# Silu's products of two strips on 64x32 tiles, results out of PSUM by ScalarE and the residual by GpSimd, in the spline layer of a four-layer network

## The chip, the cores and the metric

One core of one Trainium2 chip runs the whole program. The metric is the device time of one execution in microseconds (us); lower is better. The kernel before was timed three times, and one execution was profiled.

## What is computed

The input x is 8 images of 16 channels, 256 x 256 pixels, float32. Four layers follow each other, each of the form x = x + layer(groupnorm(x)): a capsule convolution with three rounds of routing (layer 0), a spline convolution (layer 1), attention inside 16 x 16 patches (layer 2), and a circular 3 x 3 convolution (layer 3). The change lies in layer 1, whose core is this:

```python
patches = _extract_patches(x, 3, 1, 1)          # 3x3, zero padding, x normalised
bspl = _b_splines(patches, grid)                # 8 cubic basis functions of every value
base_w = base_weight.sum(axis=2)
spl_w = (spline_weight * spline_scaler[..., None]).sum(axis=2)
out = einsum('bjhwn,ijn->bihw', silu(patches), base_w)
out = out + einsum('bjhwns,ijns->bihw', bspl, spl_w)
out = out + bias_weight[None, :, None, None]
```

So every output row needs two kinds of products with 3 x 3 weights: those of silu(x), with 16 channels, and those of the eight basis functions of x. Then a bias and the residual x are added, and the sums for the next layer's normalisation are taken.

## The kernel before, in words

**Staging.** The layers run one after another; the images between them lie in DRAM. Layer 1 (`layer1`, L851) goes over 8 images with 16 strips each; a strip is 16 rows, 128 strips in all, numbered i = 16 b + j. The result of a strip lies in one PSUM bank: four groups (n) of 32 partitions, each with 2 rows x 16 output channels, by two halves (k) of 256 pixels, so 4 x 2 x 2 = 16 rows.

**Features** (`features`, L986). A DMA fetches the rows of a strip, eight pairs of rows, into `xr`, each value four times, so that 128 partitions hold 2 rows x 16 channels x 4 shifts (L994, 1 MB). For four pairs at a time: ScalarE takes a distance to the middle of a spline and folds it (`d`, L1012, L1015); VectorE clips it twice (`a` and `e`, L1023); ScalarE squares both into PSUM (`sq`, L1029); VectorE multiplies to cubes (L1032); GpSimd subtracts the two cubes into the ring `bases` (L1041); and VectorE makes the second half, the same values kept only right of the middle (L1044). Rows outside the image are set by L1049. The ring has three places; a strip's products need its own place and the first pair of the next one. The last strip of an image has a ninth pair.

**Silu** (`silus`, L1063). Three DMAs fetch eight rows each with the 16 channels, 256 KB: `rs` twice, for the rows above and below (r = 0 and 2), and `res`, the residual (r = 1). ScalarE makes silu of both `rs` (L1082) into two of four tiles `silu`. Each holds 8 rows x 16 channels on its 128 partitions; the two together cover the rows that the strip's outputs need.

**Products** (`conv_strip`, L1098). Everything goes through the one matmul at L1106, with 32 output columns, so that four products (n = 0 to 3) go to four groups of 32 PSUM partitions. For each of two q, two kinds and three dx there are four spline products of K = 128; then three dx with four silu products (L1136), whose weights `wm` have 128 rows with zeros where a row doesn't matter for the output pair n. A float32 product is two records in the trace, so a strip has 108 spline records (some cover only half of the pixels) and 24 silu records.

**Results.** VectorE adds PSUM, bias and residual into `y`, in two halves of 256 columns (L1143), turned to the order in which layer 2 reads patches (runs of 16 pixels). It then takes the sums for the normalisation (L1155), and a DMA stores `y` (L1158).

**Order of the work.** The engines' queues are filled in program order, and that order comes from a planner written out in the kernel (`_Order`, L188). Each step is given to it with an engine, an estimated time, what it reads and writes, and a `lag` until its result is there (for DMAs); `mode="shared"` marks steps of VectorE and GpSimd that it never lets overlap; on TensorE it adds 0.25 for a change of mode. It has the number of buffers of each kind, looks at four sets of steps ahead (a set is the features of strip n, the products of strip n - 1, the silus of strip n, and what `ahead` adds), and takes the step that can start first, by rank: the set's number times the period (13.3 here) less the time to the end of its chain. Nothing of this is decided on the chip. In particular a step that waits holds back everything behind it in its engine's queue.

**The start** (`prepare`, L924). Spline weights `sw`, their scales `sc`, silu's weights `main` (nine copies to be summed) and the bias `b1` are fetched at L933 into ring places that are not used yet; VectorE scales (L937), TensorE sums over nine taps (L945 for splines, L970 for silu), VectorE finishes `tw` (L954 to L966), ScalarE copies `wm` (L982). The lags given are 10 and 16 us for these loads, 13 for the first `xr` and 6 for the others, 16 for the residual and silu rows of strip 0 and 4 for all others. In set 2 the weights of layer 2 are fetched (L1171, L1172).

**The end.** Layer 2 begins with `attend` (L1453): VectorE makes `t` (L1456) out of a patch that was loaded ahead, GpSimd adds the embedding (L1460). `t` comes from the pool `mid`, which takes over memory of layer 1's pools.

## Time and profile before

| what | value |
|---|---|
| three runs | 7644.09, 7646.63, 7649.12 us; median 7646.63 us |
| profiled execution, own time | 7643.24 us |
| its span | 7641.5 us |
| busy in the span | PE 6889.0, DVE 5415.1, ACT 2691.9, POOL 3248.8 us |
| in 5000 to 5700 us (layer 1) | PE 655.5, DVE 594.5, ACT 504.1, POOL 291.2 us, DMA 0.48 |
| layer 1's matmuls (L1106) | 4368.8 to 6132.2 us |
| one silu group of a strip | 24 records, 2.8 us |
| L1143, 128x256 | 477 ns each, two per strip |
| L1041, 128x1024 on GpSimd | 2888 ns mean |
| VectorE waiting for L1041, 4400 to 6130 us | 29.9 us |

PE is TensorE (PEld its weight loads), DVE VectorE, ACT ScalarE, POOL GpSimd and SP the engine whose queue issues most DMAs. Busy is the sum of the durations of an engine's instructions. A wait "A <- B" is time that the engine of A stood idle, ended by B. TensorE's records are pipelined, so what a group costs is read from start to start, not from durations. A duration on VectorE or GpSimd contains the time in which the instruction stood still for the other engine.

### The profile page before, as it was taken

The page shows a single profiled execution, that of the slowest core. Times are in us where ns is not written, and L with a number is a line of the kernel's source. Part 1 is how long each engine was busy: PE and PEld are TensorE (multiplying, and loading weights), DVE is VectorE, ACT ScalarE, POOL GpSimd, SP SyncE. Part 2 cuts the span into 40 slices and gives each one's busy share as a digit, 9 for nine tenths or more (in the row PEclk, how much of TensorE's full clock was granted, in tenths as well). Part 3 has the DMA queues.
Part 4 walks back from the last instruction along what each step waited for, and adds up shares of the span by engine and source line. Part 5 has one row for each costly group of instructions (what it writes and reads, how often), then busy time and mean ns, then how long its engine had stood idle before and what let it go on. Part 6 is the DMA issues. An engine that isn't in the chain of part 4 may idle for free.

```text
span 7641.5 us, 105946 instructions
## 1 busy us (share of the span) xinstructions
PE 6889.0 (90%) x43144; PEld 3276.6 (43%) x43144; DVE 5415.1 (71%) x6462; ACT 2691.9 (35%) x3835; POOL 3248.8 (43%) x1884
## 2 busy tenths in 40 slices
PE   4888888999898999998998499999999999999999
PEld 1333333333333333333333254554545566666634
DVE  5768888887888888888888688888888833333322
ACT  1222222222222222222222277777777712111200
POOL 0545555555555555555555444444444411111100
PEclk9999999999999999999999699999999999999999
DMA  6222222222222222222221344444445533333276
GB/s 243 67 65 76 77 77 77 77 77 77 77 77 77 77 77 77 77 77 76 77 76 50 105 153 156 153 152 152 154 151 161 159 114 97 86 85 97 68 214 189
DMA packets 451065, 813.01 MB, mean 106 GB/s; under 512 B 57490, under 2 KB 299282, under 8 KB 415250
## 3 DMA queue, kind: packets, MB, share of 16 engines
q1 hardware_dynamic: 380946, 738.85, 33.6%
q10 hardware_dynamic: 69632, 67.39, 3.0%
q8 instruction: 340, 5.57, 0.3%
q14 instruction: 147, 1.20, 0.1%
HBM read 595.63 MB, written 211.03 MB: 106 GB/s over the span
## 4 chain that ended last, share of the span: by engine, by line
PE 51%; POOL 21%; DVE 16%; issue 4%; ACT 3%; DMA 3%; SPq 0%; POOLq 0%; DVEq 0%; ACTq 0%
PE ps L1106 13%; POOL dd L765 11%; POOL s L765 8%; PE cv L545 8%; PE pqk L1466 6%; DVE dd L756 4%; PE p3s L1577 4%; PE cv L549 4%; PE pl L654 3%; PE po L1493 3%; PE pv L1473 3%; PE psc L1481 3%; PE fb L622 3%; DMA xr<-x1p 2%; POOL s L810 2%
## 5 line engine op out<-in xcount | busy, mean ns | idle before, releaser
L765 POOL TENSOR_TENSOR dd<-dd 128x1024 f32<-128x1024 f32 x512 | 1206.2, 2356 | 1594.9 <-DVE dd L756 1575.0
L1106 PE MATMUL ps<-bases,tw 128*32 128x512 f32 (+1 forms) x13824 | 1377.8, 550 | 109.6 <-DVE bases L1049 92.0
L756 DVE SCALAR_TENSOR_TENSOR dd<-rb,v 128x1024 f32<-128x1024 f32 (+1 forms) x1024 | 1075.2, 1082 | 206.7 <-PE rb L745 196.8
L554 ACT COPY v<-cv 128x1024 f32<-128x1024 f32 x512 | 518.2, 1012 | 1909.2 <-PE cv L549 1909.2
L1041 POOL TENSOR_TENSOR bases<-e,a 128x1024 f32<-128x1024 f32 (+1 forms) x264 | 744.9, 2823 | 1044.5 <-DVE e L1032 922.0
L545 PE MATMUL cv<-kt,w 128*128 128x512 f32 x2048 | 1090.9, 658 | 38.0 <-DVE dd L756 26.5
L1106 PEld LDWEIGHTS ps<-bases,tw 128*32 128x32 f32 x13824 | 732.4, 109 | 764.9 <-issue 458.3
L644 DVE TENSOR_TENSOR pr<-v,fb 128x2048 f32<-128x2048 f32 (+1 forms) x512 | 1019.5, 2014 | 24.9 <-PE pl L654 20.0
L745 PE MATMUL rb<-rs,ct_fold 32*128 32x512 f32 x3584 | 796.5, 658 | 8.3 <-ACT rs L727 2.7
L765 POOL TENSOR_TENSOR s<-s,dd 128x512 f32<-128x512 f32 x512 | 652.2, 1274 | 29.9
L545 PEld LDWEIGHTS cv<-kt,w 128*128 128x128 f32 x2048 | 366.1, 199 | 598.4 <-issue 389.7
L549 PE MATMUL cv<-kt,w 64*128 64x512 f32 x2048 | 590.9, 654 | 0.0
L654 PE MATMUL pl<-pr,ct_fold 128*32 128x512 f32 x3584 | 525.9, 610 | 61.0 <-DVE pr L644 60.3
L1460 POOL TENSOR_TENSOR t<-t,emb 128x512 f32<-128x512 f32 x128 | 162.1, 1266 | 961.9 <-DVE t L1456 950.8
L622 PEld LDWEIGHTS fb<-f,ct_fold 128*128 128x128 f32 x3072 | 376.7, 195 | 340.7 <-issue 296.7
L622 PE MATMUL fb<-f,ct_fold 128*128 128x128 f32 x3072 | 436.3, 290 | 90.7 <-DVE f L608 88.4
L1466 PE MATMUL pqk<-w_qk,t 128*128 128x512 f32 x1024 | 484.4, 596 | 7.6 <-POOL t L1460 7.6
L765 POOL TENSOR_TENSOR s<-v,dd 128x512 f32<-128x512 f32 x256 | 328.9, 1285 | 319.4 <-DVE dd L756 319.2
L1477 ACT ACTIVATE vt<-pv,w_b2v 128x128 f32<-128x128 f32 x512 | 146.0, 367 | 841.2 <-PE pv L1473 810.8
L1497 DVE TENSOR_TENSOR y<-po,res 128x512 f32<-128x512 f32 x128 | 88.5, 691 | 487.6 <-PE po L1493 487.6
L745 PEld LDWEIGHTS rb<-rs,ct_fold 32*128 32x128 f32 x3584 | 241.2, 188 | 380.7 <-DVE dd L756 211.7
L1032 DVE TENSOR_TENSOR e<-e,sq 128x1024 f32<-128x1024 f32 (+1 forms) x264 | 314.5, 1191 | 95.4 <-ACT sq L1029 95.4
(254 smaller groups left out, 8995.6 us busy)
## 6 DMA issues: line engine op xcount, KB each, us to landing
kt<-d SPq DMA_DIRECT2D x256, 516.0 KB
xr<-x1p SPq DMA_DIRECT2D x120, 1024.0 KB
rs<-x SPq DMA_DIRECT2D x256, 256.0 KB
d<-dn ACTq DMA_DIRECT2D x64, 516.0 KB
xs<-in_x_dram SPq DMA_DIRECT2D x16, 2048.0 KB
xs<-in_x_dram SPq DMA_DIRECT2D x64, 512.0 KB
res<-in_x_dram SPq DMA_DIRECT2D x64, 512.0 KB
x<-s SPq DMA_DIRECT2D x128, 256.0 KB
```

The lines of the kernel that those rows point to most:

```text
L545: nc.tensor.matmul(ps()[:, n], w[:, 0, j, :], t[:, a : a + 2, 0:W], start=True, stop=False)
L549: nc.tensor.matmul(ps()[:, n], w[at, 1, j, :], t[at, a : a + 2, 2 - n : 2 - n + W], start=False, stop=True)
L554: nc.scalar.copy(v[h]()[:, 4 * g : 4 * g + 4, j * W : j * W + W], ps().rearrange("p n (a w) -> p (n a) w", w=W),)
L622: nc.tensor.matmul(fb()[:, k * P : k * P + P], unfold[:, h, k, :], f()[:, 3], start=True, stop=True)
L644: nc.vector.tensor_tensor(pr()[:, :n], v[h]()[:, 4 * g : 4 * g + n], p().unsqueeze(1).to_broadcast([P, n, 512]), ALU.mult,)
L654: nc.tensor.matmul(pl()[at : at + 32], sel[:, g, h, :], pr()[:, t, :], start=h == 0 and g == 0, stop=h == 1 and (g == 1 or t == 3),)
L745: nc.tensor.matmul(r()[:, n], spread[at, g, h, :], rs()[at], start=True, stop=True)
L756: nc.vector.scalar_tensor_tensor(dd()[:, :n], r()[:, :n], 1.0 / B, v[h]()[:, a : a + n], ALU.subtract, ALU.mult)
L765: op("POOL", us, lambda: nc.gpsimd.tensor_tensor(out[0](), a[0](), b[0](), ALU.add), a[1] + b[1], out[1])
L1041: nc.gpsimd.tensor_tensor(v, rows(part(e)), rows(part(a)), ALU.subtract)
L1106: nc.tensor.matmul(out if k is None else out[:, k], lhs, rhs, start=start, stop=stop, skip_group_check=True)
L1466: nc.tensor.matmul(ps, t[:, n, k * P : (k + 1) * P], wqk[:, n, :], start=n == 0, stop=n == 1)
```

## The change

Six things, all in one edit:

1. *Silu's products in pairs of strips.* Weights `wm` are 64 rows, stored twice (partitions 0 to 63 and 64 to 127), without n: four rows of image x 16 channels are enough for a pair of output rows. At every odd strip the silu products of it and of the even strip before it are issued together: three dx with eight matmuls each, K = 64 rows by 32 columns, which alternate between the even strip's PSUM bank and the odd strip's, and between the two halves of the partitions. For the odd strip the `rs` rows are fetched with halves swapped, by two DMAs of 128 KB each, so that the two strips use opposite halves. The even strip's spline products stand before this group and the odd strip's behind it.
2. *Results.* Instead of L1143, ScalarE moves PSUM with the bias to `y` in one activation of 128 x 512, and GpSimd adds the residual in one addition of 128 x 512. The even strip's result leaves PSUM after the silu group, the odd strip's after its spline products.
3. *First loads.* The first `xr` is put ahead of the weights; the planner's costs of first loads on SP are 2.8, 3.5, 1.8 and 1.2 with lag 3 or 8 instead of 0.5 with lags of 10 to 16, and strip 0's rows have the lag of all others. `main` is a quarter as large.
4. *wm* is copied out by VectorE instead of ScalarE.
5. *Layer 2's weights* are fetched in set 6 instead of set 2.
6. *`t` of layer 2* comes from a pool of its own, opened first in layer 2.

The planner's period is 12.4 instead of 13.3. The mask `keep` for the silu rows outside the image follows the swapped halves. The core of the diff:

```diff
-            wm = one.tile([P, 3, 4, 2 * C], F32, name="wm")
+            wm = one.tile([P, 3, 2 * C], F32, name="wm")
...
-            order = _Order({**places, **banks}, 13.3)
+            order = _Order({**places, **banks}, 12.4)
...
-                sw, sc, main = at2[:, :2592], at2[:, 2592:3888], at1[:, :3456]
+                sw, sc, main = at2[:, :2592], at2[:, 2592:3888], at1[:, :864]
...
+                first = dict(sw=3.5, sc=1.8, main=1.2, b1=0.5)
                 for name, t in (("sw", sw), ("sc", sc), ("main", main), ("b1", b1)):
-                    op("SP", 0.5, lambda name=name, t=t: nc.sync.dma_start(out=t, in_=self.d[name]), [], [(name,)], lag=16.0 if name == "main" else 10.0)
+                    op("SP", first[name], lambda name=name, t=t: nc.sync.dma_start(out=t, in_=self.d[name]), [], [(name,)], lag=3.0)
...
-                op("ACT", 0.5, lambda: nc.scalar.copy(wm.rearrange("p d n m -> p (d n m)"), ps()[:, 512:896]), [(ps, 1)], [("wm",)])
+                def finish_main():
+                    nc.vector.tensor_copy(wm.rearrange("p d m -> p (d m)"), ps()[:, 512:608])
+
+                op("DVE", 0.2, finish_main, [(ps, 1)], [("wm",)], mode="shared")
...
-                op("SP", 0.5, fetch, [], [(xr, 0)], lag=6.0 if i else 13.0)
+                op("SP", 0.5 if i > 2 else 2.8, fetch, [], [(xr, 0)], lag=6.0 if i else 8.0)
+                if not i:
+                    prepare(op)
...
+                        swap = i % 2 and r != 1
+                        for at, row, n in ((0, r + 4, 4), (64, r, 4)) if swap else ((0, r, 8),):
+                            nc.sync.dma_start(
+                                out=to()[at : at + 16 * n].rearrange("p k w -> p (k w)"),
+                                in_=self.x1[j, b, :, row : row + n].rearrange("c r k w -> r c (k w)"),
+                            )
+
+                    op("SP", 0.5 if i else 0.7, fetch, [], [(to, 0)], lag=4.0)
...
+                if i % 2:
+                    both = [(open_ps.pop(k), k) for k in (i - 1, i)]
+                    keys = [("s", k, n) for k in range(2) for n in range(2)]
+                    for dx in range(3):
+
+                        def silus(dx=dx):
+                            for n in range(4):
+                                for p, k in both:
+                                    half = n // 2 ^ k % 2
+                                    at = slice(64 * half, 64 * half + 64)
+                                    src = sring[k % 2 * 2 + n % 2]
+                                    mm(n, None, wm[at, dx], src[at, :, dx : dx + W], bool(k % 2 and not dx), dx == 2 and not k % 2, p)
+
+                        op("PE", 0.9, silus, [("wm",), *keys], [(p, 0) for p, _ in both], mode="r64")
+                    evict(b, j - 1, both[0][0], op)
...
-                for dx in range(3):
-
-                    def last(dx=dx):
-                        for n in range(4):
-                            src = sring[i % 2 * 2 + n // 3]
-                            mm(n, None, wm[:, dx, n], src[:, :, dx : dx + W], stop=dx == 2)
-
-                    op("PE", 0.86, last, [("wm",), ("s", i % 2, 0), ("s", i % 2, 1)], [(ps, 0)])
+                if i % 2:
+                    evict(b, j, ps, op)
+
+            def evict(b, j, ps, op):
+                res = held.pop(b * 16 + j)
                 y = buf("y", [P, 16, 2, 16])
-                for k in range(2):
-
-                    def add(k=k):
-                        nc.vector.scalar_tensor_tensor(
-                            y()[:, :, k],
-                            ps()[:, k].rearrange("p (n j) -> p n j", j=16),
-                            b1,
-                            res()[:, k].rearrange("p (n j) -> p n j", j=16),
-                            ALU.add,
-                            ALU.add,
-                        )
-
-                    op("DVE", 0.48, add, [(ps, 0), (res, 0)], [(y, k)])
+                part = lambda ap: ap.rearrange("p k (n j) -> p k n j", j=16)
+                turned = lambda: y().rearrange("p n k j -> p k n j")
+
+                def move():
+                    nc.scalar.activation(turned(), part(ps()), AF.Identity, bias=b1)
+
+                def add():
+                    nc.gpsimd.tensor_tensor(turned(), turned(), part(res()), ALU.add)
+
+                op("ACT", 0.65, move, [(ps, 0)], [(y, 0)])
+                op("POOL", 1.3, add, [(res, 0)], [(y, 0), (y, 1)], mode="shared")
...
-                if n == 2:
+                if n == 6:
                     for name, t in self.w2.items():
...
-                if not n:
-                    prepare(op)
...
+            self.tpool = st.enter_context(tc.tile_pool(name="l2_t", bufs=2))
...
-        t = mid.tile([P, 2, 8, 32], F32, name="t")
+        t = self.tpool.tile([P, 2, 8, 32], F32, name="t")
```

## The prediction

> **What bounds the kernel now.** I read the page first, for the stages: the change touches only the spline layer and its two ends, and the stretches of the trace put that layer at 4306 to 6134 us of the span. Then four views inside it. All durations are from this one profiled execution (span 7641.5 us, own time 7643.24 us; the three timed runs have a median of 7646.63 us, so 5.1 us above its span). "Measurable" below is 0.2%, 15 us.
>
> The timeline of TensorE, over one strip in mid-image and over the step from one image to the next (start, duration, line; in brackets idle time and releaser):
>
> ```profile
> 4577.44 2.84 PE L1106 MATMUL ps<-silu,wm 128*32 128x512 f32 x24
> 4589.94 12.29 PE L1106 MATMUL ps<-bases,tw 128*32 128x512 f32 x108 [9.65 <-DVE bases L1049]
> ...
> 4630.35 10.62 PE L1106 MATMUL ps<-bases,tw 128*32 128x512 f32 x108
> 4640.65 2.88 PE L1106 MATMUL ps<-silu,wm 128*32 128x512 f32 x24
> ```
>
> A strip is 10.30 us of spline products (4630.35 to 4640.65; twelve groups of 0.86) and 2.58 us of silu products (three groups, to the next strip at 4643.23): 12.88 us. TensorE runs almost without gaps inside an image and stands still once at its start. Image 2 starts at 4589.94 and image 3 at 4811.43: 221.5 us, of which 16 x 12.88 = 206.1 is work and 15.4 is idle (9.6 at the start, the rest in small waits). So TensorE sets the pace, but narrowly. The vector side's own pace shows where TensorE had waited for it; VectorE over one strip:
>
> ```profile
> 5206.17 1.28 DVE L1044 SCALAR_TENSOR_TENSOR bases<-xr,xm,bases 128x1024 f32<-128x1024 f32 x1
> 5207.36 0.87 DVE L1143 SCALAR_TENSOR_TENSOR y<-ps,b,res 128x256 f32<-128x256 f32 x2
> 5208.27 0.69 DVE L1155 BATCH_NORM_STATS2 st<-y 128x6 f32<-128x512 f32 x1
> 5209.73 1.29 DVE L1044 SCALAR_TENSOR_TENSOR bases<-xr,xm,bases 128x1024 f32<-128x1024 f32 x1 [0.77 <-POOL bases L1041]
> ...
> 5217.98 1.28 DVE L1044 SCALAR_TENSOR_TENSOR bases<-xr,xm,bases 128x1024 f32<-128x1024 f32 x1
> ```
>
> From L1044 to L1044 is 11.81 us (5206.17 to 5217.98), only 1.07 under TensorE's 12.88. And the 0.87 us of L1143, which the change takes away, is not what holds VectorE there: it lies inside a GpSimd subtraction (L1041, 5206.42 for 3.27 us) for which VectorE waits 0.77 us more. The groups by line between 4400 and 6130 us show the two engines excluding each other:
>
> ```profile
> L1023 DVE TENSOR_SCALAR e<-d 128x256 f32<-128x256 f32 x8 | 19.6, 2449 | 0.0
> ...
> L1023 DVE TENSOR_SCALAR a<-d 128x256 f32<-128x256 f32 x8 | 2.3, 286 | 0.0
> ```
>
> The same operation on the same shape takes 286 ns, and 2449 ns when a GpSimd subtraction is running. Last, the start: ScalarE, then VectorE at the other end of the layer:
>
> ```profile
> 4305.47 0.20 ACT L351 ACTIVATE g_r<-g_r 128x1 f32<-128x1 f32 x1
> 4335.44 1.28 ACT L1082 ACT_TABLE_LOAD   x1 [29.76 <-DMA w_b2v<-in_b2v_dram]
> 4336.73 0.81 ACT L1082 ACTIVATE silu<-rs,bz,g_bc_same_lo 128x512 f32<-128x512 f32 x1
> 4337.45 1.22 ACT L1012 ACTIVATE d<-xr,bd,sd 128x1024 f32<-128x1024 f32 x1
> ...
> 6138.18 1.00 DVE L1456 TENSOR_SCALAR t<-pt,g2a_bc 128x512 f32<-128x512 f32 x2 [3.03 <-issue]
> ```
>
> ScalarE idles 30 us because a silu that needs a late load stands first in its queue; the first distance (L1012) waits behind it, and TensorE's first product comes at 4368.76.
>
> **What the Trainium skill says.** (1) "TensorE: Matmul & The Clock Gate", Part 3, Packing small matmuls: tiles on different row and column groups of the array run at the same time. The trace agrees for rows alone: in layer 0 four records of 64 x 128 (L549, 4011.30) take 1.06 us to the next start, where four full ones take 1.71 (4 x 0.43). (2) "TensorEngine Tiling (Array Packing)", Key Properties: a change of the tiling mode drains TensorE. The trace gives the price: L545 to L549 is 1.91 us for 1.71 of work, L549 to L545 1.06 for 0.86, so 0.20 each. (3) "PSUM — Partial Sum Buffer", PSUM bank collisions raise a hardware error: two row tiles may not write one bank and 32-partition quarter at once. The swapped halves keep to that (in every quarter one half writes the even strip's bank, the other the odd one's); no run here shows what such pairs cost. (4) "GPSIMD Engine Reference", Key points: GpSimd shares its SBUF interfaces with VectorE, against instructions with two SBUF inputs or in a two-port mode. The 2449 ns above agree.
>
> **Part by part.**
> - *Silu's products.* Six groups per pair of strips become three with two row tiles each: 6 x 0.86 - 3 x 0.86 = 2.58 us less, two mode changes of 0.20 more. A pair costs TensorE 2 x 10.30 + 2.58 + 0.40 = 23.58, a strip 11.79 instead of 12.88, an image 188.6 instead of 206.1: 17.5 us less. Bounds: as computed, or no overlap of rows at all (5.16 + 0.40: 0.2 more per strip). I take the overlap, since L549 shows it. Sixteen loads and products per group are no limit: L585 issues eight of each in 0.4 us.
> - *L1143 to ScalarE.* VectorE loses 0.87 (0.80 by start-to-start). ScalarE gains one activation on 512 columns from PSUM with a bias: between 0.60 (L1489, no pointer) and 0.80 (L1082, bias and scale); the skill's "ScalarE: Activation LUTs", What ACT_TABLE_LOAD costs, prices one pointer at 280 + 0.833 x 512 = 706 ns (an estimate from that page); I take 0.70. ScalarE then has 2 x 4.41 + 1.5 + 0.7 = 11.0 us per strip: hidden while the period is above that, but nearly full. Queued behind the move, which waits for TensorE, are the distances and squares; before, the two silus waited there in the same way.
> - *The residual on GpSimd.* One addition of 128 x 512, 1.27 us (L810, L1460); its 64-byte runs are new, so 1.27 to 1.6. It excludes L1023 and L1044. These are 4 x 0.60 + 2 x 1.19 = 4.8 us per strip; with GpSimd's 2 x 2.36 + 1.27 = 6.0 the shared path holds 10.8 instead of 9.5. In GpSimd's queue the next subtraction stands behind the addition, and bn_stats on VectorE waits for it. Ends for the vector pace: all of it under the multiplications L1032, 11.81 - 0.80 = 11.0; none, and L1143's going useless, 11.81 + 1.27 = 13.1. I take 12.3, a little above the middle, since 10.8 of exclusive work seldom packs into 12 us, and ScalarE at 11.0 leaves little play.
> - *Image.* The slower side sets it: 16 x 12.3 = 196.8, and at the image's end a ninth row pair and the edge rows, about 5 us of VectorE with the waits around them, so 9 (TensorE stands 9.6 there now): 205.8. Check from the other side: TensorE's 188.6 with today's 15.4 idle is 204.0. 221.5 - 205.8 = 15.7, times 8 = 126 us.
> - *First loads.* The first row load goes ahead and the weights of silu shrink from 1.73 to 0.43 MB. Today 4.8 MB land by 4320.2 (VectorE then has its scales), 14 us after the first issue; the first 1 MB alone, at the 418 GB/s of the window 4310 to 4315, is 2.5 us of transfer, and with some 3 us until its first bytes (an estimate) it is there about 6 us after 4306. ScalarE starts near 4312 instead of 4337; the weights' chain (3 MB by 4316, 2.9 + 7.2 + 5.8 us of L937, L945, L954 to L966) ends by 4332 and no longer lags. From L1012 to the first product was 31.3 us; kept, it starts 25 us sooner. Bounds 15 and 33; I take 24. The layer-2 weights moved to set 6 (five issues on SP, some 1.3 MB) fall under strips with DMA at half load: nothing, at most 3 us if they hold a row load. The four extra SP issues of a pair's split loads, 0.6 each, lie in an SP queue with over 15 us free per pair.
> - *The end.* t in its own pool need not wait for the last store (3.03 us); the last move, addition and bn_stats take 2.7 where L1143 and bn_stats took 1.6: 2 us less.
>
> Sum: 126 + 24 + 2 = 152. 7641.5 - 152 = 7489.5 in the span, 7495 as a median.
>
> **Rivals.**
> - *The shared path binds.* The addition finds no cover: 13.1 x 16 + 9 = 218.6 per image, 2.9 saved; 23 + 26 = 49 us, 7598. For: L1143 was itself hidden. Against: the order is written anew and L1032 gives 4 x 1.2 us of cover. Between it and the forecast (12.7) lies 7545.
> - *TensorE is all that counts.* 188.6 with 6 us idle: 26.9 x 8 + 26 = 241, 7405. For: pairs give slack; against: three other resources stand at 10.8 to 11.1 of 11.8.
> - *Rows don't overlap* (the change doesn't do what it says): 0.2 x 16 = 3.2 per image more, 26 in all, against 26 at the ends: 7647.
> - *Slower: GpSimd's queue blocks.* Each addition waits for the move, which waits for TensorE, and holds back the subtraction behind it: 1.27 plus about 1 us of handing over, 11.81 + 2.27 = 14.1 per strip, with 5 us at the boundary 230 per image, 8.5 more: 68 - 26 = 42, 7690. It decides from a vector pace of 13.7 on (16 x 13.7 + 5 = 224.7, 26 us over eight images, the ends' gain).
>
> **How the numbers follow.** Forecast 0.56, shared path 0.20, TensorE alone 0.12, no overlap 0.05, GpSimd's queue 0.07. Faster: 0.56 + 0.20 + 0.12 = 0.88; same 0.05; slower 0.07. The forecast's own range, paces of 12.0 to 12.8 and the start's bounds, is 7455 to 7555. The range leaves out the last two cases (0.12), half of TensorE alone and the worst end of the shared path: 7425 to 7595.
>
> **What would show it.** Three silu groups of 24 x 2 records in about 2.8 us per pair, 10.30 between; a distance between images of 204 to 207 us (today 221.5); ScalarE's first L1012 near 4312; waits of VectorE for GpSimd grown from 30 us in the layer to 100 or more. Silu groups of 5 us would mean no overlap; TensorE waiting for L1041 or L1044 in each pair, the shared path; GpSimd idle before its addition, released by ScalarE, the blocked queue. The forecast is wrong if the vector pace lies outside 11.9 to 12.9.

## The result and the profile after

The kernel after takes 7772.52 us (median of 4 runs, 7764.44 to 7779.11), the kernel before 7645.36 us beside it (7640.45 to 7649.12): a ratio of 1.0166, 95% interval 1.015 to 1.0182. The forecast was 7495 us, with a range of 7425 to 7595. The change makes the kernel slower, by 1.7%.

The profiled executions, 7641.5 us of span before and 7762.7 after, show where. The two ends went as forecast or better. The middle of layer 1, from TensorE's first product to its last, grew from 1764 to 1927 us, so from 13.8 to 15.05 us a strip.

In the code after, the clips are L1031 (were L1023), the cubes L1040 (L1032), GpSimd's subtraction L1049 (L1041), the right half of the bases L1052 (L1044), all matmuls L1119 (L1106). First the start, on ScalarE's timeline:

```profile
4310.12 2.37 ACT L1020 ACTIVATE d<-xr,bd,sd 128x1024 f32<-128x1024 f32 x2 [6.03 <-DMA res<-x]
...
4320.52 1.28 ACT L1094 ACT_TABLE_LOAD   x1 [0.33 <-DMA rs<-x]
```

The first distance comes at 4310, not 4337: the silu that waits for a late load now stands behind it. TensorE's first product comes at 4334.9 instead of 4368.8. TensorE's timeline in mid-image:

```profile
4617.60 2.81 PE L1119 MATMUL ps<-silu,wm 64*32 64x512 f32 x48
4620.34 10.54 PE L1119 MATMUL ps<-bases,tw 128*32 128x512 f32 x108
4632.88 6.21 PE L1119 MATMUL ps<-bases,tw 128*32 128x512 f32 x56 [2.00 <-POOL bases L1049]
4641.24 2.78 PE L1119 MATMUL ps<-bases,tw 128*32 128x256 f32 x30 [2.15 <-POOL bases L1049]
4644.66 2.35 PE L1119 MATMUL ps<-bases,tw 128*32 128x256 f32 x22 [0.63 <-DVE bases L1052]
```

The silu of two strips is done in 2.74 us (4617.60 to 4620.34), so the row tiles do overlap. But TensorE now stands still in nearly every pair of strips, where before it stood still for more than 2 us only at an image's start (L1049 sets the rows outside the image), and GpSimd's subtraction is what it waits for. The waits by kind between 4500 and 6000 us (engine, tile and line, what ended the wait; total us, times, longest), of the kernel before, then of the kernel after:

```profile
DVE bases L1044 <- POOL bases L1041: 26.1, 34, 0.9
PE ps L1106 <- POOL bases L1041: 2.2, 4, 0.6
PE ps L1106 <- DVE bases L1049: 58.3, 7, 9.7
```

```profile
DVE bases L1052 <- POOL bases L1049: 197.4, 130, 2.6
PE ps L1119 <- POOL bases L1049: 196.3, 79, 3.7
POOL y L1174 <- ACT y L1171: 166.3, 58, 5.9
ACT y L1171 <- PE ps L1119: 100.1, 57, 3.6
DVE st L1180 <- POOL y L1174: 59.1, 43, 3.3
```

VectorE and TensorE wait for GpSimd; GpSimd waits for ScalarE's move before its addition; ScalarE's move waits for TensorE; VectorE's statistics wait for the addition. The groups of the same stretch, each shape apart (busy us, mean ns of one, then idle time before it):

```profile
L1049 POOL TENSOR_TENSOR bases<-e,a 128x1024 f32<-128x1024 f32 x199 | 477.2, 2405 | 707.4 <-DVE e L1040 654.6 <-DMA rs<-x 31.7 <-PE ps L1119 21.1
L1052 DVE SCALAR_TENSOR_TENSOR bases<-xr,xm,bases 128x1024 f32<-128x1024 f32 x199 | 360.8, 1816 | 192.3 <-POOL bases L1049 192.3
...
L1031 DVE TENSOR_SCALAR e<-d 128x1024 f32<-128x1024 f32 x199 | 210.0, 1056 | 0.0
...
L1174 POOL TENSOR_TENSOR y<-y,res 128x512 f32<-128x512 f32 x100 | 136.0, 1360 | 166.4 <-ACT y L1171 166.3
L1171 ACT ACTIVATE y<-ps,b 128x512 f32<-128x512 f32 x100 | 68.5, 685 | 110.1 <-PE ps L1119 100.1 <-issue 6.1 <-POOL bases L1049 2.9
```

The subtraction is shorter than before (2405 ns against 2887), the right half longer (1816 against 1367), and so are half of the clips (1056 against 755). No size changed: before, GpSimd stood inside its instruction while VectorE held the path that they share; now VectorE stands inside its own. Two places in the trace, VectorE and GpSimd together, show how:

```profile
4698.26 4.69 POOL L1049 TENSOR_TENSOR bases<-e,a 128x1024 f32<-128x1024 f32 x2 [4.75 <-DVE e L1040]
4699.17 1.21 DVE L1040 TENSOR_TENSOR e<-e,sq 128x1024 f32<-128x1024 f32 x1
4700.67 3.37 DVE L1052 SCALAR_TENSOR_TENSOR bases<-xr,xm,bases 128x1024 f32<-128x1024 f32 x1 [0.29 <-POOL bases L1049]
...
4711.20 1.30 POOL L1174 TENSOR_TENSOR y<-y,res 128x512 f32<-128x512 f32 x1
4711.29 2.30 DVE L1052 SCALAR_TENSOR_TENSOR bases<-xr,xm,bases 128x1024 f32<-128x1024 f32 x1 [2.59 <-POOL bases L1049]
```

At 4698 two subtractions run back to back. The right half waits for the first of them, and when it may start, the second has taken the path: 3.37 us for an operation of 1.28. At 4711 it is the residual's addition that goes first: 2.30 us. Of the 199 right halves between 4500 and 6000 us, 31 take about 3.4 us, as at 4700, and 41 about 2.3, as at 4711; in the kernel before, 203 of 216 take about 1.3. "Trainium Architecture — The Big Picture", What this means for kernel authors, of the Trainium skill calls the path between VectorE and GpSimd an exclusive lock; these lines agree (the loser waits for the whole of the other's operation). Compare the kernel before, where the order of VectorE's queue is such that the right half is nearly always first:

```profile
5122.17 1.22 DVE L1032 TENSOR_TENSOR e<-e,sq 128x1024 f32<-128x1024 f32 x1
5123.35 1.29 DVE L1044 SCALAR_TENSOR_TENSOR bases<-xr,xm,bases 128x1024 f32<-128x1024 f32 x1
5123.56 3.32 POOL L1041 TENSOR_TENSOR bases<-e,a 128x1024 f32<-128x1024 f32 x1 [0.24 <-DVE e L1032]
```

The cube that lets the second subtraction start stands directly ahead of the right half, so VectorE goes on 0.2 us before GpSimd begins; GpSimd's subtraction takes 3.32 us, and it has time.

### The profile page after: what moved, and what is told of

It is laid out like the page before. It is cut to its first block, busy times and chain, and to the rows that moved or that the text cites. A ratio compares the mean times of both kernels' runs of the same rounds, so it can differ in the third digit from the quotient of the medians.

```text
span 7762.7 us, 106148 instructions
## 1 busy us (share of the span) xinstructions
PE 6865.4 (88%) x43144; PEld 3034.5 (39%) x43144; DVE 5493.9 (71%) x6207; ACT 2776.0 (36%) x3962; POOL 3293.2 (42%) x2012
## 5 line engine op out<-in xcount | busy, mean ns | idle before, releaser
L1119 PE MATMUL ps<-bases,tw 128*32 128x512 f32 (+1 forms) x13824 | 1477.8, 575 | 264.4 <-POOL bases L1049 250.1
L1119 PEld LDWEIGHTS ps<-bases,tw 128*32 128x32 f32 x13824 | 590.0, 114 | 1172.8 <-issue 597.7
L1049 POOL TENSOR_TENSOR bases<-e,a 128x1024 f32<-128x1024 f32 (+1 forms) x264 | 621.2, 2360 | 945.1 <-DVE e L1040 855.3
L1052 DVE SCALAR_TENSOR_TENSOR bases<-xr,xm,bases 128x1024 f32<-128x1024 f32 (+1 forms) x264 | 468.4, 1777 | 247.8 <-POOL bases L1049 247.8
```

The costliest lines, as they stand in the source:

```text
L1049: nc.gpsimd.tensor_tensor(v, rows(part(e)), rows(part(a)), ALU.subtract)
L1119: nc.tensor.matmul(out if k is None else out[:, k], lhs, rhs, start=start, stop=stop, skip_group_check=True)
```

## The experiments

Each ratio is to the runs of the kernel before on the same chip. The theories at first: G, the residual's addition on GpSimd costs the time; P, the pairs (their products and the order that the planner makes of them) do. Pace and waits below are from 4500 to 6000 us of each trace: the pace is 1500 us by half the number of right halves of 128x1024 in it, "right half" their mean, and the waits are divided by the same number of strips.

| kernel | us, median | ratio to before, 95% | us a strip | right half, ns | it waits for GpSimd, us a strip | ScalarE waits for raw rows, us a strip |
|---|---|---|---|---|---|---|
| before | 7645.36 | 1 | 13.89 | 1367 | 0.24 | 0.51 |
| after | 7772.52 | 1.0166 (1.015 to 1.0182) | 15.08 | 1816 | 1.98 | 0.41 |
| 1 VectorE's results | 7688.37 | 1.0056 (1.0041 to 1.0071) | 14.29 | 1770 | 0.73 | 1.48 |
| 2 results alone | 7990.04 | 1.0453 (1.0437 to 1.0469) | 16.85 | 2200 | 0.29 | 3.83 |
| 3 no residual | 7606.07 | 0.995 (0.9935 to 0.9965) | 13.76 | 1788 | 1.11 | 1.10 |
| 4 loads alone | 7618.86 | 0.9968 (0.9955 to 0.998) | 13.95 | 1363 | 0.25 | 0.57 |
| 5 VectorE adds | 7795.57 | 1.0199 (1.0182 to 1.0216) | 15.15 | 1320 | 1.32 | 0.16 |
| 6 fewer products | 7594.42 | 0.9935 (0.9921 to 0.995) | 13.57 | 1397 | 0.50 | 0.47 |
| 7 raw rows free early | 7628.43 | 0.9982 (0.9973 to 0.999) | 13.95 | 1779 | 0.41 | 0 |
| 8 period | 7715.87 | 1.0094 (1.0079 to 1.0109) | 14.49 | 1329 | 1.33 | 0.78 |
| 9 order kept | 7650.46 | 1.0008 (1.0001 to 1.0015) | 14.15 | 1283 | 0.87 | 2.78 |
| 10 after, order kept | 7764.3 | 1.0154 (1.0139 to 1.0169) | 14.85 | 1283 | 1.65 | 0.26 |
| 11 order kept, raw rows free | 7527.73 | 0.9852 (0.9837 to 0.9866) | 13.22 | 1283 | 0.87 | 0.01 |
| 12 rows fetched by ScalarE | 7781.82 | 1.0185 (1.0168 to 1.0202) | 15.00 | 1283 | 0.86 | 0.60 |
| 13 split fetch | 7571.94 | 0.9905 (0.989 to 0.992) | 13.57 | 1283 | 0.85 | 2.14 |
| 14 results placed | 7785.68 | 1.0186 (1.0169 to 1.0203) | 15.15 | 1289 | 0.19 | 2.72 |
| 15 loads and split fetch alone | 7602.63 | 0.9947 (0.9932 to 0.9962) | 13.76 | 1349 | 0.20 | 0.37 |
| 16 statistics later | 7761.86 | 1.015 (1.0133 to 1.0167) | 14.93 | 1728 | 1.70 | 2.81 |
| 17 the same, split fetch | 7692.71 | 1.0063 (1.0048 to 1.0078) | 14.42 | 1718 | 1.69 | 2.14 |

**1 to 4: the parts.** Number 1 is the kernel after with VectorE's two operations put back for the results:

```diff
-                op("ACT", 0.65, move, [(ps, 0)], [(y, 0)])
-                op("POOL", 1.3, add, [(res, 0)], [(y, 0), (y, 1)], mode="shared")
+                    op("DVE", 0.48, add, [(ps, 0), (res, 0)], [(y, k)])
```

> The changed kernel with only its results part undone: VectorE adds PSUM, bias and residual as before (two instructions of 128x256 per strip); pairs of silu and first loads stay. Theory G (the results part is the cause: GpSimd's addition, its handing over from ScalarE and the exclusion with VectorE lengthen the vector loop from 11.8 to 15 us per strip): 7480 to 7560 us, an image of 203 to 212 us. Rival P (the pairing is the cause: TensorE's blocks of 10 and 13 us in turn upset the vector side's order): 7700 us or more, an image of 235 us or more.

Number 2 is the kernel before with only these two operations of the change:

```diff
-                    op("DVE", 0.48, add, [(ps, 0), (res, 0)], [(y, k)])
+                op("ACT", 0.65, move, [(ps, 0)], [(y, 0)])
+                op("POOL", 1.3, add, [(res, 0)], [(y, 0), (y, 1)], mode="shared")
```

> The kernel before with only the results part of the change: ScalarE moves PSUM with the bias, GpSimd adds the residual; silu strip by strip, loads as before. G: the loss comes alone, about 20 us per image less what TensorE's own slack hid: 7720 to 7830 us. P: 7600 to 7680 us, since nothing is paired.

Number 3 is the kernel after without the addition:

```diff
-                op("POOL", 1.3, add, [(res, 0)], [(y, 0), (y, 1)], mode="shared")
```

> The changed kernel without the addition of the residual in the spline layer, which is left out (the output lacks it); the move by ScalarE stays. If the addition on GpSimd carries the loss: 7480 to 7560 us. If the move on ScalarE, behind which distances and squares wait, carries it: 7650 to 7770. P: 7700 or more.

Number 4 is the kernel before with only the first loads reordered and layer 2's weights in set 6:

```diff
-                op("SP", 0.5, fetch, [], [(xr, 0)], lag=6.0 if i else 13.0)
+                op("SP", 0.5 if i > 2 else 2.8, fetch, [], [(xr, 0)], lag=6.0 if i else 8.0)
+                if not i:
+                    prepare(op)
```

> The kernel before with only the first loads reordered and the layer-2 weights moved to set 6; silu's weights keep their full size of 1.73 MB and the results stay on VectorE. The start's gain stands by itself: 7605 to 7630 us, first product some 20 to 34 us earlier. If the vector side gives it back later: 7640 to 7650. All theories on the loss expect the same here.

The loads are worth 25 us, as said. Neither G nor P is the whole: number 1 lies between them. By steps, 7644 to 7619 for the loads, 70 up to 7688 for the pairs, 84 up to 7772 for the results. The results alone cost 346 us, more than G said: there GpSimd stands 375 us between 4400 and 6100 us waiting for ScalarE's move, and VectorE's statistics 396 us for the addition. And without the addition (number 3) 38 us are gained, little more than the two ends give: of the 140 us that the pairs take off TensorE hardly anything shows. In mid-image VectorE's order in number 3 is that of number 1 without the results, not that of the kernel after, so the 166 us between the kernel after and number 3 hold the addition and another order.

**5: who adds.** The kernel after with the residual added by VectorE:

```diff
-                    nc.gpsimd.tensor_tensor(turned(), turned(), part(res()), ALU.add)
+                    nc.vector.tensor_tensor(turned(), turned(), part(res()), ALU.add)
...
-                op("POOL", 1.3, add, [(res, 0)], [(y, 0), (y, 1)], mode="shared")
+                op("DVE", 0.7, add, [(res, 0)], [(y, 0), (y, 1)], mode="shared")
```

> The kernel after with the residual added by VectorE instead of GpSimd (the move by ScalarE stays), entered in the planner as 0.7 us in the shared mode. It parts the queue of GpSimd from the rest of the results' new path. Theory G (the addition in GpSimd's in-order queue and on the shared path is what costs): near the kernel after without the addition, 7606 us, plus 0.5 to 0.7 us of VectorE per strip, so 7640 to 7720 us. Rival H (the hand-over from TensorE by way of ScalarE to whoever adds is what costs, on any engine): 7740 us or more.

7796 us: G's number missed. H has the number, but not the reason, since number 3 has the hand-over too and takes 7606. The written order changed with it, and the loss moved from the right half (1320 ns) to the clips of `e` (1505 ns against 755). How much of the 189 us over number 3 is that order was not tested.

**6: did TensorE set the pace?** The kernel before with a third of its silu products, and everything else in its place:

```diff
-                        for n in range(4):
+                        for n in range(4 if dx == 2 else 0):
```

> The kernel before with two of its three groups of silu products per strip left out (4 of 12 matmuls stay, so the output lacks two of the three taps); the written order of every other engine is unchanged. It asks whether TensorE set the pace of layer 1 before at all. Theory T (TensorE set it, as the prediction took): 1.72 us of TensorE per strip go, and the time falls by at least 128 strips by the 1.5 us down to the vector pace that the prediction took, to 7400 to 7470 us. Theory O (the loop of the elementwise engines, through the shared path and the order, already ran at 13.8 us a strip and TensorE only waited in it): 7590 to 7640 us, and TensorE's waits for the subtraction of GpSimd grow by most of 220 us.

48 us, not 170 to 240: theory O's side, near its edge. TensorE lost 1.72 us of work a strip and the pace fell by 0.32. The rest became waiting: between 4500 and 6000 us its waits for the bases grew from 74 to 187 us, first of all that for the subtraction (2.2 before):

```profile
PE ps L1106 <- POOL bases L1041: 83.3, 59, 3.0
PE ps L1106 <- DVE bases L1049: 75.6, 7, 12.8
```

TensorE did set the pace before, but the loop of the other engines stood 0.32 us behind it. Both figures contain the starts of the images. Inside an image, from the right half of the third strip to that of the fourteenth (mean of images 2 to 8), the pace went from 13.13 to 12.90, and not to 11.8.

**7 and 8: fetches and the planner.** Number 7 is number 1 with a right half that doesn't read the raw rows:

```diff
-                        nc.vector.scalar_tensor_tensor(m, rows(xn()), xm[:, b : b + 1], v, ALU.is_gt, ALU.mult)
+                        nc.vector.scalar_tensor_tensor(m, v, xm[:, b : b + 1], v, ALU.is_gt, ALU.mult)
...
-                    op("DVE", 1.27 * us, right, [(xr, 0), ("v", i % 3, p)], [("m", i % 3, p)], mode="shared")
+                    op("DVE", 1.27 * us, right, [("v", i % 3, p)], [("m", i % 3, p)], mode="shared")
```

> The kernel with VectorE's results and pairs (first experiment), where the right half of the bases takes its comparison from the left half instead of from the raw rows, so that a buffer of raw rows is free once ScalarE has taken its distances (the comparison, and so the output, is another one; all operations keep their sizes). It tests the loop right half, free buffer of raw rows, fetch, distances. Theory X (that loop is what keeps the pairs' gain): ScalarE's wait for the raw rows falls from 186 us to under 40, and the time from 7688 to 7480 to 7580 us. Rival S (the shared path and the lockstep of VectorE and GpSimd set 13.8 us a strip whatever the fetches do): the wait for the fetches goes and others take its place; 7640 to 7700 us.

Number 8 is number 1 with the period of before:

```diff
-            order = _Order({**places, **banks}, 12.4)
+            order = _Order({**places, **banks}, 13.3)
```

> The kernel with VectorE's results and pairs (first experiment), planned with the kernel before's period of 13.3 us a strip instead of 12.4; nothing else. It shows how much of the time hangs on the written order. Theory O (the order of the elementwise work decides): the time moves by 40 us or more to either side of 7688. Rival: within 20 us of it, then the pace comes from the work and its buffers and not from how the planner ranks it.

Number 7: the wait for raw rows goes altogether, and the time falls by 60 us, just below S's range and far from X's. The right half still takes 1779 ns. Number 8: 27 us slower by one planner number, between what the two said. The order counts, but it needed a direct test.

**9 and 10: the order by itself.** VectorE's order in the trace before is, strip after strip (C clip, K cube, R right half, E results, S statistics), the first line; number 1 has the second over two strips:

```
CCC KK C KK R EE S R
CCC KKK EE R S | CCC KKK R CC R KK EE S R
```

Number 9 is number 1 with the first line written into the planner: all these steps also write one common key, `turn`, in this order (T is GpSimd's subtraction; the figure is the chunk's first row pair; `pending` holds a strip's results):

```diff
+                turns = "Ca0 Ce0 Ca4 Ka0 Ke0 T0 Ce4 Ka4 Ke4 T4 R0 E R4 Ca8 Ce8 Ka8 Ke8 T8 R8".split()
+                for k in turns:
+                    if k == "E" and pending:
+                        pending.pop(0)(op)
+                    for a, kw in put.pop(k, []):
+                        op(*a, **kw)
```

> The pairs and the first loads of the change, results on VectorE as before (the first experiment), with VectorE's order written by hand as it stood in the kernel before: per strip three clips, two cubes, a clip, two cubes, the right half of the first chunk, one strip's results and statistics, the right half of the second chunk. Only the order is changed against the first experiment (7688 us), by dependences in the planner; all work is the same. Theory O (the order that the planner makes of the pairs is what loses their gain, through the shared path): VectorE's time lost on the shared path falls from 1.1 us a strip to under 0.4 and the time to 7530 to 7600 us, the run with fewer products (7594) less 25 for the loads and 4 for the end as the middle. Rival P (the pairs cost by themselves: an even strip waits for its neighbour, results come in twos): 7650 us or more.

Number 10 is the same for the kernel after (there E is only the statistics):

> The kernel after (move by ScalarE, addition by GpSimd) with the same order by hand on VectorE: three clips, two cubes, a clip, two cubes, right half, statistics of one strip, right half. Only the order differs from the kernel after (7772 us). Theory O alone (the order is the whole loss): 7600 us or less. Rival G (the addition costs by itself, since GpSimd's queue takes it between the subtractions, behind the move, and VectorE waits): 7680 us or more, with GpSimd's waits for the move at or over 199 us. Between the two, both count.

In number 9 theory O has the mechanism right and the sum wrong. With the order kept the right half takes 1283 ns and a clip 686, so hardly anything is lost on the shared path. But of some 120 us only 38 come back, and 7650 us stands at the edge of rival P's range. Another wait has taken the place. In number 9, between 4500 and 6000 us:

```profile
ACT d L1022 <- DMA xr<-x1p: 294.3, 48, 11.5
PE ps L1128 <- POOL bases L1052: 138.7, 79, 6.2
DVE bases L1055 <- POOL bases L1052: 92.0, 106, 2.3
```

ScalarE's distances wait for the raw rows, in every second strip. In the timeline of SP's queue and ScalarE one fetch is issued at 5120.54 and the distance that needs it starts 11.9 us later:

```profile
5120.54 0.54 SPq L1000 DMA_DIRECT2D xr<-x1p  x1
...
5132.41 1.24 ACT L1022 ACTIVATE d<-xr,bd,sd 128x1024 f32<-128x1024 f32 x1 [6.33 <-DMA xr<-x1p]
```

There are three buffers of raw rows, each held from its fetch to the right half of its strip. Number 10 stays at 7764, on G's side, with 278 us of GpSimd waiting for the move (4400 to 6100 us): this is 8 us under the kernel after, with intervals that overlap. So VectorE's order alone is not what the addition costs.

**11 to 13: the raw rows.** Number 11 is number 9 with the edit of number 7.

> The kernel with the order kept (7650 us), where again the right half of the bases takes its comparison from the left half, so that a buffer of raw rows is free once ScalarE has taken its distances (the comparison, and so the output, is another one; all operations keep their sizes). In the kernel with the order kept VectorE loses nothing on the shared path any more, but ScalarE waits 338 us for raw rows. Theory X2 (the shared path and the fetch of the raw rows are two limits close to each other, and taking one away shows the other): the wait goes and the time falls by 60 us or more, to 7500 to 7590 us. Rival L (what remains is the chain of one chunk through ScalarE, VectorE and GpSimd with its three buffers, near 13.6 us a strip whatever is fetched): 7600 us or more.

Number 12 is number 9 with the silu's rows fetched by ScalarE's queue:

```diff
-                            nc.sync.dma_start(
+                            (nc.sync if r == 1 else nc.scalar).dma_start(
```

> The kernel with the order kept, where the fetches of the silu's rows are issued by ScalarE, whose own silu frees their buffers, instead of by SP. In the kernel with the order kept SP waits 410 us at these fetches for ScalarE's silu and 471 us at the stores for the results, and the fetches of the raw rows stand behind them in its queue. If SP's queue is what makes the raw rows late (theory X2): ScalarE's wait for the raw rows falls from 338 us to under 150, and the time to 7550 to 7620 us. If the buffers of the raw rows are what makes them late (rival): the wait stays over 250 us, and the time within 20 us of 7650. Issuing three fetches a strip may cost ScalarE up to 0.5 us each; then its waits move and the time rises.

Number 13 is number 9 with the raw rows in two transfers:

```diff
-                    nc.sync.dma_start(
-                        out=xr()[:, : pairs * W],
+                    for lo, hi in ((0, 4), (4, pairs)):
+                        nc.sync.dma_start(
+                            out=xr()[:, lo * W : hi * W],
```

> The kernel with the order kept (7650 us), where the raw rows of a strip are fetched in two transfers of half the rows each, so that the distances of the first chunk need only the first half. All work is the reference's. It is the loop of the raw rows shortened by its transfer, not by the buffer. Theory X2 (the transfer's 11 to 12 us between a free buffer and the distances is the second limit): the first half is there some 5 us sooner, ScalarE's wait for the raw rows falls from 338 us to 50 to 200, and the time to 7540 to 7610 us. Rival (the transfers' own rate or SP's queue, with one more issue of 0.55 us a strip, is the limit): within 25 us of 7650, or above.

Number 11 gives 7528 us, 123 below number 9; number 7, the same edit in the planner's own order, gave 60. So the shared path and the raw rows are two limits close to each other: lifting one alone gives 38 or 60 us, both together 161. This is the nearest that any run came to the forecast; it has the pairs and the loads, results on VectorE, and a comparison that isn't the reference's. So the pairs do not hold the time up by themselves (rival P of number 9). The same edit without the pairs was not run, so how much of the 161 us is theirs stays open.

In number 12 ScalarE's wait for raw rows fell from 338 to 72 us (4400 to 6100 us), but the time rose to 7782 us, since the squares now wait behind the issues:

```profile
ACT sq L1040 <- DMA x<-y: 292.6, 54, 11.6
...
5127.29 5.36 ACTq L1092 DMA_DIRECT2D rs<-x  x4
5132.70 1.03 ACT L1040 ACTIVATE sq<-a 128x1024 f32<-128x1024 f32 x1 [4.73 <-DMA x<-y]
5133.66 1.01 ACT L1040 ACTIVATE sq<-e 128x1024 f32<-128x1024 f32 x1
5133.76 1.22 DVE L1043 TENSOR_TENSOR a<-a,sq 128x1024 f32<-128x1024 f32 x1 [3.13 <-ACT sq L1040]
```

Four issues held ScalarE's queue for 5.36 us (SP took 2.37 for the same four in number 9), ahead of a square that VectorE waited for. The issues themselves are no longer than SP's: 0.52 to 0.59 us each here, a median of 0.59 over number 12 and of 0.58 for SP in number 9. Three follow each other to 5129.08; then the queue stands still for 3.05 us before the fourth. The profile puts the squares' wait down to a store; what the fourth issue waited for is not settled. As ScalarE itself came later, the fall of its wait is only a sign that SP's queue has a part in it.

Number 13 gives 7572 us, 0.9905 of before, with all the reference's work: the fastest complete kernel of these runs. The order of SP's queue is that of number 9. Yet the half comes hardly sooner than the whole did:

```profile
5112.70 1.29 SPq L1001 DMA_DIRECT2D xr<-x1p  x2
...
5124.49 1.24 ACT L1023 ACTIVATE d<-xr,bd,sd 128x1024 f32<-128x1024 f32 x1 [6.10 <-DMA xr<-x1p]
```

Over the 42 such waits of strips 16 to 111 it is 10.6 us from the issue to the distance (median), against 11.9 in number 9: 1.3 us sooner and not 5. The wait fell from 338 to 265 us, not to 200 or less. These 73 us are about the 79 us that the time fell. Why half a transfer takes nearly as long as a whole one is not shown.

**14, 16, 17: why the addition costs.** Number 14 is number 10 with the move behind the strip's four squares on ScalarE, and the addition behind both subtractions on GpSimd:

```diff
-                op("ACT", 0.65, move, [(ps, 0)], [(y, 0)])
-                op("POOL", 1.3, add, [(res, 0)], [(y, 0), (y, 1)], mode="shared")
+                op("ACT", 0.65, move, [(ps, 0), ("squares",)], [(y, 0)])
+                op("POOL", 1.3, add, [(res, 0), ("totals",)], [(y, 0), (y, 1)], mode="shared")
```

> The kernel after with the order kept on VectorE (7764 us), where also the results' two operations have a fixed place in their engines' queues: ScalarE's move behind all four squares of the strip in hand, GpSimd's addition behind both subtractions. The operations are the same. Theory Q (what the addition costs is its and the move's place in the in-order queues, ahead of squares and subtractions that VectorE waits for): VectorE's wait for the squares of the cubes falls well below its 235 us, and the time by 60 us or more, to 7640 to 7700 us. Rival W (it is the work itself: 1.3 us of the shared path and 0.7 us of ScalarE a strip): 7730 us or more.

Number 16 is number 14 with the statistics one strip later, number 17 that with the split fetch:

```diff
-                op("DVE", 0.7, measure, [(y, 0), (y, 1)], [("st", b, j), ("turn",)])
+                behind(lambda op: op("DVE", 0.7, measure, [(y, 0), (y, 1)], [("st", b, j), ("turn",)]))
```

> The kernel with the results placed (7786 us), where VectorE takes a strip's statistics one strip later, at the same spot of its queue (between the two right halves), so that they no longer wait for GpSimd's addition of the strip in hand. There VectorE waited 342 us at the statistics for the addition. The operations are the same. Theory Q2 (the addition costs by whoever waits for it in an in-order queue; with nobody behind it, it costs nothing): that wait goes and the time falls by 100 us or more, to 7690 us or less, near or under the kernel with the order kept and VectorE's results (7650). Rival W (the work itself on the shared path and ScalarE): 7730 us or more.

> The same, with the raw rows fetched in two halves: against 7572 us of the kernel with the order kept, the split fetch and VectorE's results. It has the whole of the change in it (pairs, results by ScalarE and GpSimd, first loads), with only places in queues and the fetch altered. Theory Q2: 7500 to 7590 us, since VectorE's own work is 0.95 us a strip less. Rival W: 7650 us or more.

Number 14 takes 7786 us, on rival W's side: VectorE's wait for the squares of the cubes `e` fell from 235 to 109 us, as theory Q said, but the new place put the statistics, and the right half behind them, in wait for the addition:

```profile
DVE st L1192 <- POOL y L1186: 342.4, 98, 3.5
```

Numbers 16 and 17 take that wait away, and GpSimd's wait for the move too (11.8 us instead of 278 in number 10, 4400 to 6100 us). The time still misses Q2: 7762 and 7693. Against the kernels with VectorE's results and the same fetch it is 111 and 121 us more (7650, 7572), 0.9 us a strip. Number 17's VectorE and GpSimd show where that goes; the right half is L1057 here, the subtraction L1054, the addition L1192:

```profile
5122.47 1.28 DVE L1057 SCALAR_TENSOR_TENSOR bases<-xr,xm,bases 128x1024 f32<-128x1024 f32 x1
5122.70 3.29 POOL L1054 TENSOR_TENSOR bases<-e,a 128x1024 f32<-128x1024 f32 x1 [1.29 <-DVE e L1045]
5123.66 0.69 DVE L1198 BATCH_NORM_STATS2 st<-y 128x6 f32<-128x512 f32 x1
5125.94 1.29 POOL L1192 TENSOR_TENSOR y<-y,res 128x512 f32<-128x512 f32 x1
5126.02 2.29 DVE L1057 SCALAR_TENSOR_TENSOR bases<-xr,xm,bases 128x1024 f32<-128x1024 f32 x1 [1.66 <-POOL bases L1054]
```

Number 9 has the same order with VectorE's results (L1185); its right half is L1055, its subtraction L1052:

```profile
5127.26 1.28 DVE L1055 SCALAR_TENSOR_TENSOR bases<-xr,xm,bases 128x1024 f32<-128x1024 f32 x1
5127.51 3.26 POOL L1052 TENSOR_TENSOR bases<-e,a 128x1024 f32<-128x1024 f32 x1 [1.36 <-DVE e L1043]
5128.45 0.87 DVE L1185 SCALAR_TENSOR_TENSOR y<-ps,b,res 128x256 f32<-128x256 f32 x2
5129.36 0.69 DVE L1197 BATCH_NORM_STATS2 st<-y 128x6 f32<-128x512 f32 x1
5130.81 1.28 DVE L1055 SCALAR_TENSOR_TENSOR bases<-xr,xm,bases 128x1024 f32<-128x1024 f32 x1 [0.76 <-POOL bases L1052]
```

In this order VectorE has nothing else to do while GpSimd subtracts. With the results on VectorE, 0.87 us of this time were theirs, and the wait left was 0.76. Without them the wait is 1.66: the work taken off VectorE has turned into idle time. Then the addition, ready at the same moment, takes the path ahead of the second right half, which needs 2.29 us instead of 1.28. So it is in 90 of the 104 strips between 4500 and 6000 us. One microsecond lost a strip, nothing won: rival W's side, and the mechanism is in the trace.

**15.** The kernel before with the loads of number 4 and the split fetch:

> The kernel before with the reordered first loads (7619 us) and the raw rows fetched in two halves as in the run beside it; nothing of the pairs or the results. If the fetch was already a limit of the kernel before (theory X2 says that it was near, its wait was 55 to 60 us in layer 1): 7560 to 7610 us. If not: within 10 us of 7619.

7603 us lies in the first range, but its interval and that of number 4 touch (0.9932 to 0.9962, 0.9955 to 0.998): a gain of some 16 us, not settled. With the order kept and the fetch split, the pairs (with the smaller parts of the change that number 9 keeps) are worth 31 us (7603 to 7572) of the 140 that they take off TensorE.

## Why the prediction was wrong

**Silu's products: right.** 2.58 us were forecast for the three groups and 0.20 for each change of mode; 2.74 us were measured from the first group's start to the next spline product.

**L1143 to ScalarE: the price right, the gain wrong.** The move takes 685 ns (forecast 700). But the 0.87 us taken off VectorE were credited towards the lower end of the vector pace, though the prediction had itself read that the operation "lies inside a GpSimd subtraction". Number 17 shows that in its order they became waiting. That is no rule: number 3, whose order in mid-image is number 1's, has the move and no addition, and takes 82 us less than number 1 (0.64 a strip).

**The residual on GpSimd: duration right, cover wrong.** 1360 ns, inside 1.27 to 1.6. The prediction put part of it under the cubes. In number 17 it lies on a right half in nearly every strip; in the kernel after also between GpSimd's subtractions, behind a move that waits for TensorE. Without the addition (number 3) the kernel takes 166 us less: 1.30 us for each of 128 strips, about its own duration (1.29 in number 17, 1.36 here), though the order is another one too. Where it is lost, the lines of number 17 show for that order only.

**The vector pace: the step that failed.** "I take 12.3", between 11.0 and 13.1, inside an image. Read as under number 6, the pace there is 15.25 us (13.13 before). The base was mis-sized: 11.81 from one right half to another was read from one strip in which VectorE waited only once, 0.77 us for GpSimd. With TensorE's load lightened in the kernel before (number 6) the other engines' pace inside an image was 12.90. So in that order they stood 0.23 us a strip behind TensorE, not 1.07. Over whole images the forecast counted on 0.98 us a strip (221.5 less 205.8, over 16), and number 6 gave 0.32. The credit for L1143 and the cover for the addition, the other two terms, failed as said above. And all ends assumed that the rest would keep its order. The pairs' results and the new period made the planner write another one, in which right halves lose the path to a second subtraction or to the addition: 1816 ns against 1367. No term of the sum stood for that. What it costs in the kernel after is open: number 10 has right halves of 1283 ns and takes about as long.

**The image** (205.8 us, measured 240.8 or 16 strips of 15.05) follows from it.

**First loads: right.** 24 us forecast, 25 alone (number 4); the first distance at 4310, forecast near 4312. In the kernel after the first product even comes 34 us sooner. **The end:** 2 forecast; from the last product to layer 2's first it is 3.9 us instead of 7.6. What made the other 1.7 us was not taken apart.

**The rivals.** The shared path was named with the right sign, priced at 13.1 a strip for one more addition, without the order. GpSimd's blocked queue, the slower one, is there too (166 us of waiting for the move, in 58 places between 4500 and 6000 us), and the pace of 13.7 from which it was to decide was reached by other causes too (its own sum has a slip: 16 x 13.7 + 5 is 224.2, not 224.7). Number 16 takes that wait away, and the time hardly changes: so it wasn't the one mechanism either. What stays open is how the 163 us more of the layer's middle divide between order, shared path and queue in the kernel after itself, since each takes the other's place when it is lifted; and why half a fetch comes hardly sooner than a whole one.

## What to carry to other kernels

The pace of an engine is not what its best strip shows: lighten the engine ahead of it, with the order kept, and see how far the time falls before a gain there is counted. Work that fills a wait costs nothing where it is (0.87 us of results in number 9); moved to the engine that is waited for, it can cost nearly its whole length (0.9 us a strip for an addition of 1.29 in numbers 16 and 17). And where a planner writes the order, a change of one step's cost rewrites all queues, so compare the order of the queues before the durations.

## What the runs showed of the hardware

- A right half of 1.28 us takes 3.37 when GpSimd has a second subtraction ready at the end of the first, and GpSimd's subtraction of 2.4 takes 3.3 when VectorE is 0.2 us earlier. Which engine loses was decided by who was first by a fraction of a microsecond, and so by the order of the queues.
- Eight matmuls with K = 64, alternating between the two row halves and two PSUM banks, take the time of four with K = 128: 2.74 us for 24 against 2.58 for 12.
- A DMA issue took 0.59 us in ScalarE's queue (number 12) and 0.58 in SP's (number 9), medians of 300 and 316. But four in ScalarE's queue held it for 5.36 us where SP's four took 2.37: the last of them was issued 3.05 us after the third had ended.
- The first half of a transfer of 1 MB was used 10.6 us after its issue, the whole one after 11.9 (medians, numbers 13 and 9).
